# A hybrid attention and state-space layer on one core: the order of TensorE and ScalarE work tied in all blocks of the mixer

## The chip, the cores and the metric

The kernel runs on one core of a Trainium2 chip, in one launch. The metric is the device time of that launch in microseconds, the median of three runs. A core has five engines that run their own instruction streams and meet at semaphores: TensorE (PE; matrix products and transposes, results in PSUM), VectorE (DVE), ScalarE (ACT; functions such as exp and silu, each from a table that an ACT_TABLE_LOAD brings in), GpSimd (POOL), and SyncE (SP), which here issues loads.

## The reference, cut to what matters

The input is x of 4 sequences x 256 positions x 512 channels. Four layers are added to it in turn: attention with an adapter, a gated feed-forward layer, a state-space mixer, and the feed-forward layer again. The change concerns the mixer alone. Cut to its core, the reference of the mixer is

```python
H, P, N, G, K, CS = (128, 64, 128, 8, 4, 32)      # INTER = H * P = 8192
proj = input_states @ in_proj_w.T
gate, xBC, dt = split(proj)
xBC = silu(conv1d(xBC, conv_w, depthwise, K = 4) + conv_b)
hs, Bm, Cm = split(xBC)
A = -exp(A_log); dt = clip(softplus(dt + dt_bias), 0)
cum = cumsum(dt * A)
Ldec = where(i >= j, exp(cum[i] - cum[j]), 0)
scores = einsum('bcihn,bcjhn->bcijh', Cc, Bc) * Ldec * dt
y = einsum('bcijh,bcjhp->bcihp', scores, xc) + (states carried over) + D * hs
g = y * silu(gate)
g = g * rsqrt(mean over a group(g * g) + eps) * norm_w
out = g @ out_w.T
```

The kernel doesn't walk in chunks of 32 with a carried state. It takes the sum over all earlier positions of a sequence at once, with 256 positions as two halves of 128, and so needs, for each head and sequence, three 128 x 128 pieces of decays: first half on itself, second half on the first, second half on itself.

## The kernel before, in words

The mixer has 128 heads of 64 channels. Two heads make a block of 128 channels: 64 blocks (NB). Eight blocks (GB) make a group (G = 8), which shares one pair of projections B and C and one normalisation. All 1024 positions (NT) lie in the free dimension.

Block i of group g, with gi its place in the group, does this:

- `projected("x", i)` (TensorE) multiplies one 128-channel slice of the weights with the input, in two halves of 512 positions. Each half is 4 x 3 matmuls, since `mm3` (lines 110 to 117) makes a float32 product of three products of split parts. The result `pp` lies in PSUM, in a pool of two buffers that x, gate, B and C projections take in turn.
- `conv` (lines 961 to 976): ScalarE writes the bias and one tap from `pp` to `acc` (964), VectorE adds three taps (971), which are the last readers of that `pp`, and ScalarE takes the silu in place (975).
- `projected("g", i)` is the gate, whose silu is `gt` (1219). One `gt` buffer exists.
- `rows` loads a head's cumulated decays from DRAM to all partitions (tile `r`), and `differences` (from 999) makes the three pieces of decays of a head in a tile `em`: four VectorE subtractions (1004), a select on GpSimd (1008), and nine exponentials on ScalarE (1013, 1014, 1016). There are three `em` buffers and a block takes two.
- `weighted` (1020) multiplies `em` with the group's scores `gm` on VectorE.
- `turned` transposes x on TensorE (`trx`, 1027) and scales it by dt on VectorE (`xd`, 1030).
- `product` (1044) multiplies `em` and `xd` to `pyy`, and `gated` (1054, 1057, 1061) adds D x, multiplies with the gate, squares for the norm, and stores the block to DRAM (`spill`).

`scores` (from 977) makes `gm` of a group from its B and C, a sequence at a time, with a PSUM tile `pg` (986, 990) and a VectorE product (991). B and C of the next group are projected in the fourth and fifth block of a group (`NEXT`).

The output product of a group (`recall`, `partial`, `scaled`; tiles `gr`, `gh`, `pog`) is done while the next group runs: eight pieces of 128 positions, 24 matmuls each, dealt to its blocks by the table PER (at the end of block gi, PER[gi + 1] pieces are recalled, and the block after does their products in `outer`).

`trx`, `pg`, `pog` and the sums `pqs` share one PSUM pool of two buffers (tag "m").

What sets the order: each engine's instructions are put in order when the kernel is built, by a scheduler with its own estimate of times. Inside `tc.manual_schedule(engines={nc.tensor.engine})` TensorE keeps the order of the program. Before the change this holds for blocks 8 to 63; the first group and the end after the last block are left to the scheduler. `tc.issue_after(ins)` puts what follows behind `ins` on `ins`'s engine, without a wait between engines.

In a block, TensorE's written order is: first half of x(i), the transposes of block i - 1 (`turn`), second half of x(i), then the product of block i - 1 either at once, or, where `late` is set, between the two halves of the gate's projection.

Of the kernel before, what the change touches and what calls it, by code (L numbers as in the profile page):

```python
# [20 lines left out]
P = 128  # L21
# [12 lines left out]
EPS = 1e-5  # L34

NEXT = {3: "b", 4: "c"}


COLS = {}
# [40 lines left out]
def hybrid_kernel(  # L80
# [705 lines left out]
    def mixer(feed, later):  # L786
        with ExitStack() as es, ExitStack() as inner:
# [168 lines left out]
                    nc.tensor.transpose(tr[:, q, :], dt[:, q * P : (q + 1) * P], ident)  # L956
                nc.scalar.activation(dt_t[:, qs, :], tr, AF.Relu)

            silus = []

            def conv(pp, ch, tag, bufs):

                acc = (po_ if tag == "gb" else p2).tile([P, NT], F32, name="acc", tag=tag, bufs=bufs)
                nc.scalar.activation(  # L964
                    acc, pp, AF.Identity, bias=cb_s[:, ch : ch + 1], scale=cw_s[:, ch, 3:4]
                )
                av = acc.rearrange("p (b t) -> p b t", b=B)
                pv = pp.rearrange("p (b t) -> p b t", b=B)
                for tap in range(3):
                    d = 3 - tap  # L970
                    nc.vector.scalar_tensor_tensor(  # L971
                        av[:, :, d:], pv[:, :, : L - d], cw_s[:, ch, tap : tap + 1], av[:, :, d:],
                        ALU.mult, ALU.add,
                    )
                silus.append(nc.scalar.activation(acc, acc, AF.Silu).ins)
                return acc

            def scores(bt, ct):

                gm = p2.tile([P, B, 3, P], F32, name="gm", tag="gm", bufs=1)  # L980
                yield gm
                for b in range(B):
                    pg = ps.tile([P, 3, P], F32, name="pg", tag="m")
                    k0, k1 = bt[:, b * L : b * L + P], bt[:, b * L + P : (b + 1) * L]
                    q1 = ct[:, b * L + P : (b + 1) * L]
                    nc.tensor.matmul(
                        pg[:, 0:2, :].rearrange("p s i -> p (s i)"), k0, ct[:, b * L : (b + 1) * L],
                        start=True, stop=True,
                    )
                    nc.tensor.matmul(pg[:, 2, :], k1, q1, start=True, stop=True)  # L990
                    nc.vector.tensor_tensor(gm[:, b], pg, tri.rearrange("p (s i) -> p s i", s=3), ALU.mult)
                    yield

            def rows(h):
                r = p2.tile([P, NT], F32, name="r", tag="r", bufs=3)
                load(r, cumd[h : h + 1, :].to_broadcast([P, NT]))
                return r

            def differences(h, r):
# [13 lines left out]
                    nc.scalar.activation(e[:, b, 1, :], rv[:, b, 1, :], AF.Exp, bias=col_t[:, h, b, 2:3])  # L1013
                nc.scalar.activation(e[:, :, 2, :], e[:, :, 2, :], AF.Exp)
                for b in range(B):
                    nc.scalar.activation(e[:, b, 0, :], rv[:, b, 0, :], AF.Exp, bias=col_t[:, h, b, 0:1])  # L1016
                return e

            def weighted(e, gm):
# [77 lines left out]

            def recall(g, t, half):

                r = po_.tile([P, 4, P], F32, name="gr", tag="gr", bufs=3)  # L1100
                s = [po_.tile([P, 4, P], F32R, name=f"gh{j}", tag=f"gh{j}", bufs=3) for j in range(2)]
                ts = slice(t * P, (t + 1) * P)
                n = 3 if half == 1 and g == G - 1 else 4
# [43 lines left out]
            def convolved(kind, g):  # L1147
                at_ = NB if kind == "b" else NB + G
                group[kind] = conv(projected(kind, g), at_ + g, "gb", 3)
# [13 lines left out]
                py = product(xd, em)  # L1163
                sqs[m // GB] = gated(m, px2, gt, py, sqs.get(m // GB))

            convolved("b", 0)
            convolved("c", 0)
            scoring = scores(group["b"], group["c"])
            gm = next(scoring)
            for _ in range(B):  # L1170
                next(scoring)
            rr = {h: rows(h) for h in range(2)}
            stage, sqs, wos, rgs, todo = {}, {}, {}, {}, []
            recalled = []
            PER = {1: 1, 2: 2, 3: 1, 4: 1, 5: 2, 6: 1}
            def block(i, scoring, gm):
                g, gi = divmod(i, GB)
                if gi == 0 and g:
                    scoring = scores(group["b"], group["c"])
                    gm = next(scoring)  # L1180
                    todo.extend((g - 1, t) for t in range(TT))

                def scored():

                    for _ in range(2 if gi == 0 and g else 0):
                        next(scoring)

                def turn():

                    if i - 1 in stage and len(stage[i - 1]) == 3:  # L1190
                        px2, pgt, pem = stage[i - 1]
                        stage[i - 1] = px2, pgt, turned(i - 1, px2), pem

                x2 = conv(projected("x", i, turn), i, "x2", 2)

                late = gi in (7, 0, 1) and g > 0
                if not late:
                    if recalled:  # L1200
                        outer()
                    if i:
                        inner_products(i - 1)
                    while recalled:
                        outer()
                if gi == 6:
                    wos.setdefault(g, []).extend(out_weights(g, k) for k in range(3))

                def between():
                    scored()  # L1210
                    if late:
                        inner_products(i - 1)
                        while recalled:
                            outer()

                pp = projected("g", i, between)
                scored()
                gt = p2.tile([P, NT], F32, name="gt", tag="gt", bufs=1)
                nc.scalar.activation(gt, pp, AF.Silu)
                em = []  # L1220
                for h in (2 * i, 2 * i + 1):
                    with tc.issue_after(silus[2]) if i == 0 else ExitStack():
                        em.append(differences(h, rr.pop(h)))
                    if h + 2 < H:
                        rr[h + 2] = rows(h + 2)
                xd = [turned(i, x2)] if g == 0 else []
                if gi in NEXT and g + 1 < G:
                    convolved(NEXT[gi], g + 1)
                for e in em:
                    weighted(e, gm)  # L1230
                stage[i] = (x2, gt, *xd, em)
                for _ in range(PER.get(gi + 1, 0)):
                    if todo:
                        q, t = todo.pop(0)
                        recalled.append((q, t, [recall(q, t, half) for half in range(2)]))
                if gi == 7:
                    wos[g].extend(out_weights(g, k) for k in range(3, 6))
                if gi == 0 and g:
                    wos[g - 1].extend(out_weights(g - 1, k) for k in range(6, 8))
                return scoring, gm  # L1240

            for i in range(GB):
                scoring, gm = block(i, scoring, gm)
            with tc.manual_schedule(engines={nc.tensor.engine}):
                for i in range(GB, NB):
                    scoring, gm = block(i, scoring, gm)
            px2, pgt, pem = stage[NB - 1]
            stage[NB - 1] = px2, pgt, turned(NB - 1, px2), pem
            inner_products(NB - 1)
            wos[G - 1].extend(out_weights(G - 1, k) for k in range(6, 8))  # L1250
            es_p.close()
            ps_o = pool("m_o", 4, space=PSUM, **freed)
            pos = {}
# [118 lines left out]
```

## Time and profile before

| what | value |
|---|---|
| median of 3 runs | 1888.84 us (1888.56 to 1890.16) |
| the profiled execution, whole | 1889.63 us |
| its span, first to last instruction | 1887.9 us |
| granted TensorE clock, mean | 0.986 |
| table loads on ScalarE in the mixer's silus and exponentials | 60 (line 975), 58 (1219), 49 (1013), 40 (1014), 23 (1016), 1283 ns each |
| first and last product of a block (line 1044) | 426.1 and 1802.3 us |

The profile is of one execution, so its lines are to be set against 1889.63 and not against the median. The span has three stretches: attention and feed-forward up to about 370 us, the mixer's blocks from about 415 to 1803 us, and the last output products with the second feed-forward layer after that. TensorE is called PE, and its weight loads PEld. A busy TensorE means that matmuls are in its pipeline; the ends of matmuls are modelled. In a timeline, the number in brackets is the idle time of that engine before the instruction, and the name after it is what released it. A matmul of 512 columns is shown with 0.39 us, but in a row they start 0.2275 us apart, and in the same way VectorE and ScalarE operations in a row overlap a little, so that start-to-start times are shorter than the durations.

### The profile page before, as it was taken

The page shows a single profiled execution, that of the slowest core. Times are in us where ns is not written, and L with a number is a line of the kernel's source. Part 1 is how long each engine was busy: PE and PEld are TensorE (multiplying, and loading weights), DVE is VectorE, ACT ScalarE, POOL GpSimd, SP SyncE. Part 2 cuts the span into 40 slices and gives each one's busy share as a digit, 9 for nine tenths or more (in the row PEclk, how much of TensorE's full clock was granted, in tenths as well). Part 3 has the DMA queues.
Part 4 walks back from the last instruction along what each step waited for, and adds up shares of the span by engine and source line. Part 5 has one row for each costly group of instructions (what it writes and reads, how often), then busy time and mean ns, then how long its engine had stood idle before and what let it go on. Part 6 is the DMA issues. An engine that isn't in the chain of part 4 may idle for free.

```text
span 1887.9 us, 29843 instructions
## 1 busy us (share of the span) xinstructions
PE 1814.7 (96%) x10706; PEld 1459.8 (77%) x10706; DVE 1470.2 (78%) x2272; ACT 1456.8 (77%) x2876; POOL 465.8 (25%) x425
## 2 busy tenths in 40 slices
PE   8999988899999999999999999999999999999997
PEld 6777767677778887888788878877887888788786
DVE  5566667788888788877878787869787878888767
ACT  6666675379998879887988797879778977988843
POOL 6332230024441122113211311222132222211200
PEclk9999999899999999999999999999999999999999
DMA  4000000035555445543654454546444644554321
GB/s 143 1 1 1 22 15 26 24 102 167 162 181 189 138 145 176 181 143 122 206 156 151 140 185 154 159 125 205 145 146 151 189 140 145 174 176 159 109 91 45
DMA packets 152772, 240.35 MB, mean 127 GB/s; under 512 B 12464, under 2 KB 77616, under 8 KB 152624
## 3 DMA queue, kind: packets, MB, share of 16 engines
q1 hardware_dynamic: 143552, 205.41, 35.1%
q10 hardware_dynamic: 9072, 33.03, 4.5%
q8 instruction: 84, 1.38, 0.3%
q14 instruction: 64, 0.52, 0.1%
HBM read 202.75 MB, written 35.65 MB: 126 GB/s over the span
## 4 chain that ended last, share of the span: by engine, by line
PE 76%; ACT 9%; DVE 8%; issue 3%; POOL 2%; DMA 2%; SPq 0%; ACTq 0%; DVEq 0%; POOLq 0%
PE pp L115 12%; PE pp L116 12%; PE pp L117 11%; PE pyy L1044 9%; PE pog L115 6%; PE pog L116 6%; PE pog L117 6%; PE trx L1027 2%; ACT e L477 2%; DVE acc L971 2%; PE ptr L493 1%; PE pq L115 1%; PE pq L116 1%; PE pq L117 1%; DVE eT L494 1%
## 5 line engine op out<-in xcount | busy, mean ns | idle before, releaser
L115 PE MATMUL pp<-mx,w 128*128 128x512 f32 (+1 forms) x1160 | 463.8, 400 | 4.7 <-DVE acc L971 3.0
L117 PE MATMUL pp<-mx,w 128*128 128x512 f32 (+1 forms) x1160 | 451.9, 390 | 0.0
L116 PE MATMUL pp<-mx,w 128*128 128x512 f32 (+1 forms) x1160 | 451.8, 390 | 0.0
L971 DVE SCALAR_TENSOR_TENSOR acc<-pp,cw_s,acc 128x1012 f32<-128x1012 f32 (+2 forms) x240 | 304.6, 1270 | 47.3 <-ACT acc L964 45.9
L1020 DVE TENSOR_TENSOR em<-em,gm 128x1536 f32<-128x1536 f32 x128 | 229.4, 1792 | 98.8 <-ACT em L1016 94.9
L1008 POOL TENSOR_SCALAR_AFFINE_SELECT r<-r 128x512 f32<-128x512 f32 x128 | 133.0, 1039 | 647.4 <-DMA r<-cumd 553.3
L115 PEld LDWEIGHTS pp<-mx,w 128*128 128x128 f32 x1160 | 218.3, 188 | 58.4 <-issue 7.6
L117 PEld LDWEIGHTS pp<-mx,w 128*128 128x128 f32 x1160 | 218.3, 188 | 46.0 <-issue 0.3
L116 PEld LDWEIGHTS pp<-mx,w 128*128 128x128 f32 x1160 | 218.8, 189 | 40.7 <-issue 0.6
L1068 POOL TENSOR_TENSOR sq<-sq,acc 128x1024 f32<-128x1024 f32 x55 | 147.6, 2684 | 310.7 <-ACT acc L1061 282.6
L115 PE MATMUL pog<-wo,gh 128*128 128x512 f32 x512 | 203.5, 397 | 0.0
L116 PE MATMUL pog<-wo,gh 128*128 128x512 f32 x512 | 200.3, 391 | 0.0
L117 PE MATMUL pog<-wo,gh 128*128 128x512 f32 x512 | 199.9, 390 | 0.0
L1044 PE MATMUL pyy<-em,xd 128*64 128x256 f32 (+1 forms) x2048 | 191.4, 331 | 4.2 <-DVE em L1020 3.0
L1044 PEld LDWEIGHTS pyy<-em,xd 128*64 128x64 f32 x2048 | 135.8, 138 | 64.5 <-issue 20.9
L1004 DVE TENSOR_SCALAR em<-r,col_t 128x128 f32<-128x128 f32 x512 | 169.9, 386 | 14.3 <-PE pyy L1044 13.5
L1013 ACT ACTIVATE em<-r,col_t 128x128 f32<-128x128 f32 x512 | 167.3, 392 | 17.6 <-PE pyy L1044 15.1
L1016 ACT ACTIVATE em<-r,col_t 128x128 f32<-128x128 f32 x512 | 165.4, 388 | 0.3
L107 ACT CAST w<-wr 128x512 fp32r<-128x512 f32 x144 | 88.1, 612 | 69.5 <-PE pp L116 56.4
L1030 DVE TENSOR_TENSOR xd<-trx,dt_t 128x512 f32<-128x512 f32 x128 | 83.2, 683 | 64.9 <-PE trx L1027 64.8
L107 ACT CAST gh<-gr 128x512 fp32r<-128x512 f32 (+1 forms) x128 | 76.7, 605 | 58.4 <-PE pog L116 46.3
L477 ACT ACTIVATE e<-sc,nmx 128x256 f32<-128x256 f32 (+1 forms) x256 | 104.0, 441 | 21.0 <-DVE nmx L471 20.9
(290 smaller groups left out, 3335.3 us busy)
## 6 DMA issues: line engine op xcount, KB each, us to landing
wr<-in_win_dram SPq DMA_DIRECT2D x287, 256.0 KB, 2.8
r<-cumd SPq DMA_DIRECT2D x128, 512.0 KB, 4.1
spill<-gb ACTq DMA_DIRECT2D x63, 512.0 KB, 2.8
gr<-spill SPq DMA_DIRECT2D x120, 256.0 KB, 3.0
wor<-in_wout_dram SPq DMA_DIRECT2D x64, 256.0 KB, 4.0
out_dram<-x SPq DMA_DIRECT2D x8, 256.0 KB, 2.3
x<-in_x_dram SPq DMA_DIRECT2D x1, 1536.0 KB, 8.9
gr<-spill SPq DMA_DIRECT2D x8, 192.0 KB, 2.5
```

Of the source, the lines that this page charges most:

```text
L107: nc.scalar.copy(hl[0], v)
L115: nc.tensor.matmul(o, lh, rh, start=(first and k == 0), stop=False)
L116: nc.tensor.matmul(o, lh, rl, start=False, stop=False)
L117: nc.tensor.matmul(o, ll, rh, start=False, stop=(last and k == n - 1))
L477: nc.scalar.activation(es_[c][:, 2 * j + pr, :], sc[:, j, :], AF.Exp, bias=nm[:, j : j + 1], accum_out=rs[:, c, h : h + 1],)
L971: nc.vector.scalar_tensor_tensor(av[:, :, d:], pv[:, :, : L - d], cw_s[:, ch, tap : tap + 1], av[:, :, d:], ALU.mult, ALU.add,)
L1004: nc.vector.tensor_scalar(e[:, b, 2, :], rv[:, b, 1, :], col_t[:, h, b, 1:2], 0.0, ALU.subtract, ALU.min,)
L1013: nc.scalar.activation(e[:, b, 1, :], rv[:, b, 1, :], AF.Exp, bias=col_t[:, h, b, 2:3])
L1016: nc.scalar.activation(e[:, b, 0, :], rv[:, b, 0, :], AF.Exp, bias=col_t[:, h, b, 0:1])
L1020: nc.vector.tensor_tensor(e, e, gm, ALU.mult)
L1044: nc.tensor.matmul(py[d, b, k * P :], xd[:, 2 * b + k, d], es2[hh][:, b, 2 * k : 2 if k == 0 else 3, :].rearrange("p s i -> p (s i)"), sta ...
L1068: (nc.gpsimd if n < NB - 1 else nc.vector).tensor_tensor(sq, sq, x2, ALU.add)
```

## The change

- All 64 blocks are now under the written order on TensorE, the first group included.
- On ScalarE, the exponentials of block i (both heads) are issued behind the gate's silu of block i - 1; the silu of x(i), with the silu of a B or C made in the block before, behind the last exponential; the gate's silu of block i behind that. `decays(i)` with the loads of the next rows is called ahead of x(i)'s projection.
- The scores of the next group are made in block gi = 6 (the seventh) of a group, two sequences after x's projection and two after the gate's, into one of now two `gm` buffers. Before, they were made in the first block of their group.
- `r` and `gr` go from three to two buffers each.
- In the first group every product is `late`; in the last group the eighth block's is not.
- The last group's turn at output products of the group before follows a new table, LAST: one piece in each block, and the eighth after the last block (`outer()` behind the loop).

```diff
+PER = {1: 1, 2: 2, 3: 1, 4: 1, 5: 2, 6: 1}
+LAST = {1: 1, 2: 1, 3: 1, 4: 1, 5: 1, 6: 1, 7: 1, 8: 1}
...
-            silus = []
+            silus, exps = [], []
+
+            def silu(acc):
+                silus.append(nc.scalar.activation(acc, acc, AF.Silu).ins)
...
-                silus.append(nc.scalar.activation(acc, acc, AF.Silu).ins)
                 return acc
...
-                gm = p2.tile([P, B, 3, P], F32, name="gm", tag="gm", bufs=1)
+                gm = p2.tile([P, B, 3, P], F32, name="gm", tag="gm")
...
-                r = p2.tile([P, NT], F32, name="r", tag="r", bufs=3)
+                r = p2.tile([P, NT], F32, name="r", tag="r", bufs=2)
...
-                    nc.scalar.activation(e[:, b, 0, :], rv[:, b, 0, :], AF.Exp, bias=col_t[:, h, b, 0:1])
+                    exp = nc.scalar.activation(
+                        e[:, b, 0, :], rv[:, b, 0, :], AF.Exp, bias=col_t[:, h, b, 0:1]
+                    )
+                exps.append(exp.ins)
...
-                r = po_.tile([P, 4, P], F32, name="gr", tag="gr", bufs=3)
+                r = po_.tile([P, 4, P], F32, name="gr", tag="gr", bufs=2)
...
+            gms = {}
+
+            def scored(g, n):
+
+                if g == G:
+                    return
+                if g not in gms:
+                    scoring[g] = scores(group["b"], group["c"])
+                    gms[g] = next(scoring[g])
+                for _ in range(n):
+                    next(scoring[g])
...
+            def decays(i):
+                em = []
+                for h in (2 * i, 2 * i + 1):
+                    em.append(differences(h, rr.pop(h)))
+                    if h + 2 < H:
+                        rr[h + 2] = rows(h + 2)
+                return em
+
+            def block(i):
                 g, gi = divmod(i, GB)
+                per = PER if g < G - 1 else LAST
...
+                if i:
+                    with tc.issue_after(silus[-1]):
+                        em = decays(i)
+                x2 = conv(projected("x", i, lambda: turn(i - 1) if i else None), i, "x2", 2)
+                with tc.issue_after(exps[-1]) if i else ExitStack():
+                    for acc in [x2, *unsilued]:
+                        silu(acc)
+                unsilued.clear()
+                if i == 0:
+                    with tc.issue_after(silus[-1]):
+                        em = decays(i)
+                if gi == 6:
+                    scored(g + 1, 2)
 
-                late = gi in (7, 0, 1) and g > 0
+                late = g == 0 or (gi in (7, 0, 1) and g < G - 1) or gi < 2
...
                 pp = projected("g", i, between)
-                scored()
+                if gi == 6:
+                    scored(g + 1, 2)
                 gt = p2.tile([P, NT], F32, name="gt", tag="gt", bufs=1)
-                nc.scalar.activation(gt, pp, AF.Silu)
-                em = []
-                for h in (2 * i, 2 * i + 1):
-                    with tc.issue_after(silus[2]) if i == 0 else ExitStack():
-                        em.append(differences(h, rr.pop(h)))
-                    if h + 2 < H:
-                        rr[h + 2] = rows(h + 2)
-                xd = [turned(i, x2)] if g == 0 else []
+                with tc.issue_after(silus[-1]):
+                    silus.append(nc.scalar.activation(gt, pp, AF.Silu).ins)
                 if gi in NEXT and g + 1 < G:
                     convolved(NEXT[gi], g + 1)
+                    unsilued.append(group[NEXT[gi]])
                 for e in em:
-                    weighted(e, gm)
-                stage[i] = (x2, gt, *xd, em)
-                for _ in range(PER.get(gi + 1, 0)):
+                    weighted(e, gms[g])
+                stage[i] = (x2, gt, em)
+                for _ in range(per.get(gi + 1, 0)):
...
-            for i in range(GB):
-                scoring, gm = block(i, scoring, gm)
             with tc.manual_schedule(engines={nc.tensor.engine}):
-                for i in range(GB, NB):
-                    scoring, gm = block(i, scoring, gm)
-            px2, pgt, pem = stage[NB - 1]
-            stage[NB - 1] = px2, pgt, turned(NB - 1, px2), pem
+                for i in range(NB):
+                    block(i)
+            outer()
+            turn(NB - 1)
             inner_products(NB - 1)
```

## The prediction

> **What bounds the kernel now.** I read the page's busy shares first, then TensorE's own table of waits, then the timelines of TensorE, VectorE and ScalarE around one group start (904 to 930 us), last the end of the block loop.
>
> ```profile
> span 1887.9 us, 29843 instructions
> PE 1814.7 (96%) x10706; PEld 1459.8 (77%) x10706; DVE 1470.2 (78%) x2272; ACT 1456.8 (77%) x2876; POOL 465.8 (25%) x425
> ```
>
> TensorE is the bound. From 919.04 to 1098.43 us, one group of eight blocks (179.4 us), it is busy 178.1 us, ScalarE 148.2, VectorE 147.8. Its waits in the mixer are few:
>
> ```profile
> PE pg L986 <- DVE gm L991: 8.6, 7, 1.4
> PE pyy L1044 <- DVE em L1020: 3.0, 3, 2.2
> PE pp L115 <- DVE acc L971: 3.0, 4, 1.5
> ```
>
> The columns are total us, times, longest. The first is the seven group starts, where the scores wait for the single gm. All TensorE gaps over 0.05 us from 418 us to the loop's end add up to about 19 us: 8.6 there, 5.4 in the first group, 4.6 in the last block, the rest tiny. That is all that better order could win directly.
>
> Now a group start (block 24), ScalarE, then VectorE, then TensorE:
>
> ```profile
> 911.62 1.20 ACT L964 ACTIVATE acc<-pp,cb_s,cw_s 128x1024 f32<-128x1024 f32 x1
> ...
> 916.94 1.26 ACT L1013 ACTIVATE em<-r,col_t 128x128 f32<-128x128 f32 x4
> 918.11 0.97 ACT L1016 ACTIVATE em<-r,col_t 128x128 f32<-128x128 f32 x3
> 919.10 1.28 ACT L975 ACT_TABLE_LOAD   x1
> ```
>
> ```profile
> 917.25 1.27 DVE L971 SCALAR_TENSOR_TENSOR acc<-pp,cw_s,acc 128x1020 f32<-128x1020 f32 x1
> ...
> 919.37 1.27 DVE L1054 SCALAR_TENSOR_TENSOR gb<-acc,dh,pyy 128x1024 f32<-128x1024 f32 x1
> ```
>
> ```profile
> 912.05 2.82 PE L1044 MATMUL pyy<-em,xd 128*64 128x256 f32 x32
> ...
> 919.04 0.70 PE L986 MATMUL pg<-acc 128*128 128x256 f32 x2 [1.21 <-DVE gm L991]
> ...
> 920.37 0.48 PE L115 MATMUL pp<-mx,w 128*128 128x512 f32 x1
> ```
>
> The reader is to see an order: the bias of x's convolution (911.62) comes before the second head's exponentials, which wait for the product of the block before (912.05 to 914.80). So the last convolution tap, begun at 917.25, is over at 918.5, before TensorE wants that PSUM buffer for the next block's x (920.37).
>
> [...] a load from 907.76 is followed by an exponential at 909.06. [...] after the 2.20 us gap before 1798.15 the clock is 0.50 in 1798.6 to 1802.0, and at 1793 us matmuls stand 0.43 us apart, not 0.227.
>
> **The change, part by part.** I took instruction order from the built program, durations from the trace. Rn is block n's transposes, Yn its product.
>
> (a) Table loads fall from 262 to 165: 97 x 1.283 = 124 us of ScalarE. I count 0: ScalarE has 31 us to spare in a group, and after the first group no TensorE wait for it in the block loop exceeds 0.1 us until the last block.
>
> (b) Scores in block 6 with two gm, their VectorE products (0.55 us each) moving along: the waits go, -8.6. The first product of a group also ran 3.40 us instead of 2.75 (929.63 to 933.03) on late weighted exponentials: 7 x 0.65 = -4.5. New: the scores share two PSUM buffers with transposes and out products, and stand behind weighted multiplies on VectorE. By hand gm is ready within 0.2 us of need: +1.5 for seven (0 to +7).
>
> (c) The decisive part. Each block takes two of three em buffers, so a block's second head waits for the preceding product. At blocks 16, 24, 32, 40, 48 and 56 the built ScalarE order is now (block 16; em_8113 is its second head, acc_8178 its convolution):
>
> ```
> 721 L1019 Activation em_8113<-r_7962,col_t_4980 128x128 x4
> 722 L1020 Activation em_8113<-em_8113 128x4x128
> 723 L1022 Activation em_8113<-r_7962,col_t_4980 128x128 x4
> 724 L111 TensorCopy w0_8136<-wr_7966 128x512
> 725 L971 Activation acc_8178<-pp_8140,cb_s_4737,cw_s_4735 128x1024
> ```
>
> So the convolution's bias, and a weight cast for the next x, are queued behind exponentials that wait for Y15, and Y15 stands in the middle of g16. VectorE has the same inversion: second head's differences, gated, first head's weighting, a weight's low part, the gate's multiply, and only then the taps. TensorE's x17 takes x16's PSUM buffer, so it waits for the third tap. Counted from Y15's end, in back-to-back starts of the VectorE timeline: 0.1 semaphore (898.40 to 898.50 between Y's end and an exponential); differences 0.87; gated 1.19; weighting 1.67; low part 0.60; multiply 1.14; tap 1.19; low part 0.60; tap 1.19; weighting 1.67; tap 1.27 = 11.5 us. ScalarE stays inside this: exponentials 1.18 + 0.52 + 1.27, cast 0.5, bias 1.2 end at 4.8; tap one starts at 5.6. TensorE has only g16's second half, 12 x 0.2275 = 2.7 us. Stall 8.7 us, six times: +52. R16's silu (tap, load 1.28, silu 1.06: 13.9) is then in time, x17's half ending at 14.3. Block 8 keeps the bias ahead and is counted in (e).
>
> (d) [...] 6 x 1.6 = +9.6 (0 if the clock holds[...]).
>
> (e) First group, now tied. Before: gaps 5.4 us, and seven products cut after two matmuls, each restart about 0.4: -8 in all. After, the third tap stands behind the second head's differences: in block 2 x3 waits 4.2 us (0.97 + tap 1.19 + gated 1.19 + tap 1.19 + multiply 1.14 + tap 1.27 = 7.0, less 2.7); by the same sums block 8 3.7, block 7 1.9, block 6 1.7 (there R6 waits for gm), and Y0 about 1 without filling matmuls. +12.5[...]. Net +7 (-5 to +15).
>
> (f) The end. An out product now covers the last silu: -1.4 - 1.1 - 2.2, and the two half-clock windows there -3.2. The last product still waits for its transposes scaled on VectorE behind weight work, about +1.2[...]. Net -5.
>
> (g) r from three to two buffers, gr likewise. A row is free when its exponentials end, about 11 us before the next use; landing takes a median 4.1 us and the select 1.04. gr lands in 3.0. Rows and selects move up with the exponentials. On SP a row's load waits for exponentials and holds weight loads behind it, which are wanted a block later; on POOL square sums (2.68 us) stand behind selects that wait for rows, and the next reader of their tile comes some 10 us later. I take 0 (0 to +10). Silus behind exponentials reach R at 5.5 us after Y in blocks with 5.56 us of cover: +1 in all (0 to +10).
>
> Sum: -8.6 - 4.5 + 1.5 + 52 + 9.6 + 7 - 5 + 1 = +53. The profiled execution took 1889.63 us (span 1887.9 and 1.7 around it): 1942.6. The median, 1888.84, is 0.8 lower: I say 1942.
>
> **Rivals.** *Faster:* the tie works as named, with no inversion. Then (c), (d) and (e)'s stalls vanish and -8.6 - 4.5 + 1.5 - 5 - 8 + 1 = -24: about 1866. For it: TensorE waits on little else, and ScalarE gains 124 us. Against: the listed order, em's three buffers. It decides if x17's wait after Y15 is under 3 us, for then six waits are under 18 us. *Stalls without the clock, cheap first group:* drop (d), (e) at 0: 53 - 17 = +36, about 1925. [...] *More waits:* the tight silus and the two-buffer loads of (g) at their upper ends[...]: +53 + 9 + 10 + 9 = +81, 1970. Against: 8 to 14 us of cover in most blocks. *The tie does nothing:* excluded for order, since the built orders differ; but equal time would need gains and stalls to cancel, 2%.
>
> **How the numbers follow.** Forecast 0.71, stalls without clock 0.14, more waits 0.08, faster 0.05, same 0.02. The range, 1918 to 1964, takes the forecast with (d) and (e) at their bounds and the second rival, and leaves most of the third and all of the faster one out. What a measurement can tell from no change is 0.2%: faster 0.05, same 0.02, slower 0.93.
>
> **What would show it.** TensorE's waits should name the convolution taps (pp from acc) with six waits near 8.7 us, each at a group's second x; the clock should read a half just after; pg's wait should be gone; ACT_TABLE_LOADs should be 165 and ScalarE's busy time near 1330. Wrong if those six waits are short: then the order of execution or the buffer's owner isn't what I read. Groups of 179.4 us should become about 188.

## The result, and the profile after

| | us | ratio to before, 95% interval |
|---|---|---|
| before, median of 4 runs (the three above and one more) | 1888.70 (1886.68 to 1890.16) | |
| after, median of 4 runs | 1952.26 (1949.57 to 1955.48) | 1.0338 [1.0317, 1.0359] |
| after, the profiled execution (span 1948.4) | 1950.19 | |

The change costs 63.6 us. The forecast was 1942, its range 1918 to 1964. The page's busy shares first:

```profile
span 1948.4 us, 29707 instructions
PE 1816.9 (93%) x10706; PEld 1461.4 (75%) x10706; DVE 1487.7 (76%) x2272; ACT 1330.1 (68%) x2779; POOL 448.2 (23%) x425
```

TensorE does the same 10706 matmuls in nearly the same busy time (2.2 us more), so nearly all of the loss is idleness. ScalarE is busy 127 us less and nothing is gained by it. TensorE's table of waits (total us, times, longest):

```profile
PE pp L119 <- DVE acc L978: 71.4, 10, 10.3
PE trx L1036 <- DVE gm L997: 4.3, 2, 2.4
...
PE pog L119 <- DVE gm L997: 1.9, 6, 0.3
```

The wait for gm ahead of the scores is gone; projections now wait for the taps of a convolution (978). Six of the ten are at x(17), x(25), ... x(57), 10.1 to 10.3 us each. Timelines around the first of them, ScalarE, then VectorE (whole from 741.44 on), GpSimd and TensorE:

```profile
741.44 1.29 ACT L1019 ACTIVATE em<-r,col_t 128x128 f32<-128x128 f32 x4 [0.78 <-PE pyy L1053]
742.63 0.62 ACT L1020 ACTIVATE em<-em 128x512 f32<-128x512 f32 x1
743.15 1.28 ACT L1022 ACTIVATE em<-r,col_t 128x128 f32<-128x128 f32 x4
744.33 0.61 ACT L111 CAST w<-wr 128x512 fp32r<-128x512 f32 x1
744.84 1.21 ACT L971 ACTIVATE acc<-pp,cb_s,cw_s 128x1024 f32<-128x1024 f32 x1
```

```profile
741.44 0.88 DVE L1010 TENSOR_SCALAR em<-r,col_t 128x128 f32<-128x128 f32 x4 [1.17 <-PE pyy L1053]
742.23 1.28 DVE L1063 SCALAR_TENSOR_TENSOR gb<-acc,dh,pyy 128x1024 f32<-128x1024 f32 x1
743.42 1.75 DVE L1029 TENSOR_TENSOR em<-em,gm 128x1536 f32<-128x1536 f32 x1
745.09 0.69 DVE L112 TENSOR_TENSOR w<-wr,w 128x512 fp32r<-128x512 f32 x1
745.69 1.22 DVE L1066 TENSOR_TENSOR gb<-gb,gt 128x1024 f32<-128x1024 f32 x1
746.83 1.27 DVE L978 SCALAR_TENSOR_TENSOR acc<-pp,cw_s,acc 128x1012 f32<-128x1012 f32 x1
748.01 0.68 DVE L112 TENSOR_TENSOR w<-wr,w 128x512 fp32r<-128x512 f32 x1
748.61 1.27 DVE L978 SCALAR_TENSOR_TENSOR acc<-pp,cw_s,acc 128x1016 f32<-128x1016 f32 x1
749.79 3.32 DVE L1029 TENSOR_TENSOR em<-em,gm 128x1536 f32<-128x1536 f32 x1
753.04 1.27 DVE L978 SCALAR_TENSOR_TENSOR acc<-pp,cw_s,acc 128x1020 f32<-128x1020 f32 x1
```

```profile
749.16 2.34 POOL L1077 TENSOR_TENSOR sq<-sq,acc 128x1024 f32<-128x1024 f32 x1
```

```profile
743.96 0.39 PE L121 MATMUL pp<-mx,w 128*128 128x512 f32 x1
754.45 0.77 PE L119 MATMUL pp<-mx,w 128*128 128x512 f32 x1 [10.10 <-DVE acc L978]
755.02 0.63 PE L120 MATMUL pp<-mx,w 128*128 128x512 f32 x1
```

The reader is to see the inversion in two queues. On ScalarE the second head's exponentials wait for Y15 (released at 741.44 by pyy), and the bias of x(16) stands behind them (744.84), although the matmuls of x(16) were over before 736 and ScalarE stood idle for 0.78 us just ahead of 741.44. On VectorE the three taps stand behind and between seven other operations, 9.2 us from start to start, of which the first waits for Y15 too. VectorE doesn't pause until the last tap ends at 754.3, and the bias was over at 746.05, 0.8 us ahead of the first tap: so it is VectorE's queue that sets the length of the stall. Had the taps (3.6 us) followed the bias at once, the last would have ended at about 749.7; by this estimate from the lines above ScalarE's order alone would still leave some 5 of the 10.1 us. TensorE is out of work at 744.35 and idles for these 10.1 us. Behind the wait its matmuls take 0.63 us instead of 0.39, at a granted clock of 0.50 up to 758.8.

The span in sections, by the ends of the products (us; Yn is block n's product):

| | to the mixer | Y0 to Y8 | six groups, Y8 to Y56 | Y56 to Y63 | Y63 to the end |
|---|---|---|---|---|---|
| before | 407.8 | 142.1 | 179.4 to 179.7 | 151.7 | 85.2 |
| after | 402.4 | 151.3 | 189.4 to 190.8 | 142.9 | 85.3 |

The 24.4 us from the start of the mixer to Y0 are the same in both. The six groups bring +65.5, the first +9.2, the last stretch -8.8. The 5.4 us ahead of the mixer are not the change's: over all profiles of this study that stretch took 401.8 to 407.8 us with the same code.

### The profile page after: what moved, and what is told of

It reads as the page before. It is cut to its first block, busy times and chain, and to the rows that moved or that the text cites. A ratio compares the mean times of both kernels' runs of the same rounds, so it can differ in the third digit from the quotient of the medians.

```text
span 1948.4 us, 29707 instructions
## 1 busy us (share of the span) xinstructions
PE 1816.9 (93%) x10706; PEld 1461.4 (75%) x10706; DVE 1487.7 (76%) x2272; ACT 1330.1 (68%) x2779; POOL 448.2 (23%) x425
## 4 chain that ended last, share of the span: by engine, by line
PE 74%; DVE 12%; ACT 7%; issue 3%; DMA 2%; POOL 2%; SPq 0%; DVEq 0%; ACTq 0%; POOLq 0%
PE pp L119 12%; PE pp L120 11%; PE pp L121 11%; PE pyy L1053 8%; PE pog L119 6%; PE pog L120 6%; PE pog L121 6%; DVE acc L978 3%; PE trx L1036 2%; ACT e L481 2%; DVE em L1029 2%; PE ptr L497 1%; PE pq L119 1%; DVE em L1010 1%; PE pq L120 1%
## 5 line engine op out<-in xcount | busy, mean ns | idle before, releaser
L119 PE MATMUL pp<-mx,w 128*128 128x512 f32 (+1 forms) x1160 | 472.3, 407 | 72.6 <-DVE acc L978 71.4
L120 PE MATMUL pp<-mx,w 128*128 128x512 f32 (+1 forms) x1160 | 458.8, 396 | 0.0
L121 PE MATMUL pp<-mx,w 128*128 128x512 f32 (+1 forms) x1160 | 457.9, 395 | 0.0
L119 PEld LDWEIGHTS pp<-mx,w 128*128 128x128 f32 x1160 | 222.7, 192 | 126.7 <-issue 76.7
L1014 POOL TENSOR_SCALAR_AFFINE_SELECT r<-r 128x512 f32<-128x512 f32 x128 | 119.8, 936 | 765.2 <-DMA r<-cumd 588.3
L1029 DVE TENSOR_TENSOR em<-em,gm 128x1536 f32<-128x1536 f32 x128 | 238.7, 1865 | 43.1 <-ACT em L1022 42.6
L121 PEld LDWEIGHTS pp<-mx,w 128*128 128x128 f32 x1160 | 222.8, 192 | 47.9
L120 PEld LDWEIGHTS pp<-mx,w 128*128 128x128 f32 x1160 | 223.4, 193 | 41.3
L1077 POOL TENSOR_TENSOR sq<-sq,acc 128x1024 f32<-128x1024 f32 x55 | 136.5, 2482 | 264.3 <-ACT acc L1070 264.3
L1053 PE MATMUL pyy<-em,xd 128*64 128x256 f32 (+1 forms) x2048 | 180.5, 329 | 0.7 <-DVE xd L1039 0.7
L1053 PEld LDWEIGHTS pyy<-em,xd 128*64 128x64 f32 x2048 | 128.1, 137 | 60.3 <-issue 18.3
L1010 DVE TENSOR_SCALAR em<-r,col_t 128x128 f32<-128x128 f32 x512 | 146.1, 342 | 25.8 <-PE pyy L1053 22.9
L112 DVE TENSOR_TENSOR gh<-gr,gh 128x512 fp32r<-128x512 f32 (+1 forms) x128 | 103.2, 815 | 44.0 <-ACT gh L111 44.0
```

The source lines that it names most:

```text
L119: nc.tensor.matmul(o, lh, rh, start=(first and k == 0), stop=False)
L120: nc.tensor.matmul(o, lh, rl, start=False, stop=False)
L121: nc.tensor.matmul(o, ll, rh, start=False, stop=(last and k == n - 1))
L1010: nc.vector.tensor_scalar(e[:, b, 2, :], rv[:, b, 1, :], col_t[:, h, b, 1:2], 0.0, ALU.subtract, ALU.min,)
L1014: nc.gpsimd.affine_select(rv[:, :, 0, :], rv[:, :, 0, :], pattern=[[0, B], [1, P]], compare_op=ALU.is_ge, fill=-1e30, base=0, channel_mult ...
L1029: nc.vector.tensor_tensor(e, e, gm, ALU.mult)
```

## The experiments

The sums named below are those six. Each ratio is to executions of the kernel before that were taken along with the run (medians 1888.25 to 1890.34), and each "theory" is one that the expectation of that run names. For the reading, the mean interval from one product's end to the next, by place in the group (groups 2 to 6 counted from 0; place 0 is from Y15 to Y16, place 7 from Y14 to Y15, and likewise in the other groups):

| us | 0 | 1 | 2 to 4, each | 5 | 6 | 7 |
|---|---|---|---|---|---|---|
| before | 18.29 | 24.76 | 25.63 | 25.63 | 17.47 | 16.42 |
| after | 27.36 | 24.76 | 25.63 | 27.56 | 18.83 | 14.77 |
| scores alone | 18.27 | 24.77 | 25.63 | 27.26 | 18.83 | 15.13 |
| both heads behind the conv | 15.40 | 25.27 | 25.63 | 27.55 | 18.83 | 19.64 |
| the same, old scores | 16.13 | 24.76 | 25.63 | 25.63 | 17.47 | 20.65 |
| the same, no ties | 16.45 | 24.76 | 25.63 | 25.63 | 17.47 | 18.23 |
| 43 filling products | 25.35 | 24.76 | 25.63 | 27.66 | 18.83 | 14.75 |

**1. The second head's exponentials behind the conv.**

```diff
-                        em = decays(i)
+                        em = decays(i, (0,))
                 x2 = conv(...)
+                bias, tap = convs[-1]
+                if i:
+                    with tc.issue_after(bias), tc.issue_after(tap), tc.issue_after(exps[-1]):
+                        em += decays(i, (1,))
```

> The changed kernel, with one thing moved: the second head's exponentials (and its clamp and its mask) are built behind the same block's conv bias and last tap instead of ahead of them. The ties between exponentials and silus, the scores in block 6, the two-buffer r and gr and the new dealing of out products stay; 206 table loads instead of 165. In blocks 16, 24, ... 56 only the gated sum of the product before still stands between two taps. Theory 1 (the inversion is the loss: a stall of 10.1 us and about 2 us of halved clock at each of six places): the wait ahead of the next x projection falls from 10.1 to about 1.6 us, the clock stays full there, and the six sums of eight blocks fall from 190.5 to about 180 us: 1880 to 1890 us in all, level with the kernel before. Theory 2 (the ties, or fewer buffers for r and gr, or a tighter order in general cost the time): the six sums stay above 187 us and the time above 1930.

Measured: 1973.59 us, 1.0451 [1.0429, 1.0473]; six sums 191.5 to 193.7. The 10 us wait is gone, but 2.2, 1.1, 1.4 and 4.0 us came at four places nearby. By its numbers theory 2 came true, but the run was no clean test: the first head's exponentials, still called ahead, keep the bias behind them, and 41 table loads came on top. ScalarE's timeline, and the same 16 us in the windows of this run and of the kernel before (columns: busy TensorE, weight loads, VectorE, ScalarE, GpSimd, then clock, DMA share, GB/s):

```profile
753.06 1.28 ACT L1020 ACTIVATE em<-r,col_t 128x128 f32<-128x128 f32 x4
...
755.93 1.19 ACT L971 ACTIVATE acc<-pp,cb_s,cw_s 128x1024 f32<-128x1024 f32 x1
```

```profile
744.00:760.00 16.00, 12.83 (x77) 9.36 (x76) 9.54 (x9) 15.90 (x30) 3.02 (x3) 0.97 0.58 165
```

```profile
744.00:760.00 16.00, 15.95 (x96) 12.75 (x95) 16.00 (x21) 15.92 (x31) 3.68 (x2) 1.00 0.76 236
```

The projection of x(16) was over about 749, its bias began at 755.93. ScalarE is full in both kernels here; before, TensorE doesn't wait, as the bias comes early in the queue. Order decides here, not ScalarE's busy share.

**2. The taps in a row as well.**

```diff
+                with tc.issue_after(convs[-1][1]) if m < NB - 1 else ExitStack():
-                sqs[m // GB] = gated(m, px2, gt, py, sqs.get(m // GB))
+                    sqs[m // GB] = gated(m, px2, gt, py, sqs.get(m // GB))
```

> As the run with the second head's exponentials behind the conv, and besides, the gated sum of the product before is tied behind the last tap of the block's x conv on VectorE, so that nothing stands between the taps of blocks 16, 24, ... 56; 233 table loads. Theory 1 (the inversion is the whole loss): no wait before the six x projections, sums of eight blocks of 178 to 179 us, 1868 to 1880 us in all: faster than the kernel before, by what the other parts of the change bring. Theory 2 (ties, buffers or lost freedom of order): above 1930 us. In between, at 1885 to 1930, both carry a part.

Measured: 1966.38 us, 1.0413 [1.0389, 1.0437]; six sums 188.1 to 190.6. By its numbers theory 2 again. Waits of 1.2, 1.0 and 5.1 us are left around Y15. The 5.1 us are at x(17), where the bias (756.44) still stands behind the first head's exponentials (the last four from 754.76). Moving one head is no cure, even with the taps together.

**3. Both heads behind the conv.** A clean test: TensorE's order is unchanged.

```diff
-                if i:
-                    with tc.issue_after(silus[-1]):
-                        em = decays(i)
                 x2 = conv(projected("x", i, lambda: turn(i - 1) if i else None), i, "x2", 2)
+                if i:
+                    with tc.issue_after(silus[-1]):
+                        em = decays(i)
```

> The changed kernel with one call moved: both heads' exponentials are called behind the x conv of their block instead of ahead of it. Ties, scores in block 6, two-buffer r and gr and the dealing of out products stay, TensorE's order is the same to the instruction, there are 166 table loads for 165. In blocks 16, 24, ... 56 the conv bias now stands ahead of both heads' exponentials on ScalarE and the three taps stand in a row on VectorE. (The earlier run with the second head alone moved was no clean test: it left the first head's nine exponentials ahead of the bias and added 41 table loads.) Theory 1 (the inversion in six blocks is what costs): no waits of 10 us, the six sums 179 to 182 us, 1870 to 1892 us in all. Theory 2 (the ties or the two-buffer tiles cost): six sums above 187 us, above 1935 us. Between: both.

Measured: 1909.06 us, 1.0116 [1.0101, 1.0131]; six sums 183.0 to 184.6. TensorE's waits:

```profile
PE trx L1036 <- ACT acc L966: 26.5, 13, 3.6
PE pp L119 <- DVE acc L978: 5.0, 7, 1.0
```

The waits for taps fall from 71.4 to 5.0 us and 43 us are won. That is most of the loss, but the kernel stays 21 us above before: between the theories. What comes late now is the silu of x (966), which the tie puts behind all exponentials.

**4. The old place of the scores, with both heads behind the conv.**

```diff
-                if gi == 6:
-                    scored(g + 1, 2)
+                if gi == 0 and g:
+                    scored(g, 2)
```

(at both places, with one gm and three r and gr)

> As the run with both heads' exponentials behind the conv, and the scores put back where the kernel before has them (a group's first block, one buffer for gm, three for r and gr); 178 table loads. If moving the scores costs about 2 us a group, as it did alone on the kernel before: 8 to 14 us below the run with both heads behind the conv. If in the company of the ties the move does bring the waits for gm: 5 to 12 us above it.

Measured: 1894.21 us, 1.0035 [1.0023, 1.0047], 14.9 us less than experiment 3. So the moved scores cost, together with the two-buffer r and gr that go with them. In the table of intervals places 5 and 6, where the moved scores were, shrink by 1.9 and 1.4 us, and 7 and 0 grow by 1.0 and 0.7. The first group is 5.3 us shorter.

**5. The scores moved, alone on the kernel before.**

```diff
-                if gi == 0 and g:
+                if gi == 6 and g + 1 < G:
                     scoring = scores(group["b"], group["c"])
...
-                    for _ in range(2 if gi == 0 and g else 0):
+                    for _ in range(2 if gi == 6 and g + 1 < G else 0):
```

(two gm, two r and gr; half of the scores ahead of the out products, as in the change)

> The kernel before with one part of the change alone: a group's scores computed in the seventh block of the group before (two buffers for gm, two instead of three for r and gr). Theory 1 (as the prediction's step on the scores has it): the waits for gm and the slow products behind them in the first block of a group go, 8.6 us and 4.5 us, about 1.5 us of small waits come: 11 us less, about 1877 us. Theory 2 (two buffers for r and gr, or two score products ahead of the out products, take it back): 1886 us or more.

Measured: 1901.59 us, 1.0062 [1.0050, 1.0075]: 11.3 us slower, theory 2 and the opposite of the prediction's step. TensorE's timeline at the group start:

```profile
740.65 0.47 PE L115 MATMUL pp<-mx,w 128*128 128x512 f32 x1 [1.43 <-DVE acc L971]
748.60 0.50 PE L115 MATMUL pp<-mx,w 128*128 128x512 f32 x1 [1.13 <-ACT gt L1222]
```

The wait for gm (1.2 us) went, and these two came. In the table of intervals, places 5 and 6, where TensorE never waited, grow by 1.63 and 1.36 us, the scores' own matmuls; place 7 gives back 1.29; place 0 gives nothing. The two new waits are for VectorE and ScalarE, so around the group start TensorE is held by these, and the scores had been filling that time. Fewer buffers for r and gr went along and weren't tried apart.

**6. The old place of the scores in the changed kernel.** The same edit, on the changed kernel.

> The changed kernel with only the scores put back where the kernel before has them (one buffer for gm, three for r and gr); 159 table loads. The conv bias of block 16 then stands ahead of the second head's exponentials, but in block 17 all nine exponentials of the second head, which wait for block 16's product, stand ahead of block 17's bias. Theory 1 (the early call of the exponentials makes an inversion, wherever the order puts it): a wait of about 10 us moves one block on, to the projection x(18), x(26), ...; 1930 to 1955 us. Theory 2 (moving the scores is what makes the stall): no wait above 3 us, under 1905 us.

Measured: 1914.56 us, 1.0151 [1.0131, 1.0170]: neither theory.

```profile
PE pp L119 <- DVE acc L978: 31.7, 11, 5.4
```

No 10 us wait is left. TensorE waits for taps 2.0 us at x(17) and not at all at x(18), where theory 1 had the stall, so theory 1 is refuted there. But the first group takes 159.4 us (before 142.1), and five waits for taps of 1.0 to 5.4 us, 18.7 of the 31.7, lie in it. With the old scores ScalarE has the bias of block 16 (748.66) ahead of the second head's exponentials (750.27) again: the inversion there takes the early call together with the moved scores and the buffers that go with them.

**7. The ties removed, the early call kept.** The three `issue_after` inside the blocks are left out.

```diff
-                    with tc.issue_after(silus[-1]):
-                        em = decays(i)
+                    em = decays(i)
...
-                with tc.issue_after(exps[-1]) if i else ExitStack():
-                    for acc in [x2, *unsilued]:
-                        silu(acc)
+                for acc in [x2, *unsilued]:
+                    silu(acc)
...
-                with tc.issue_after(silus[-1]):
-                    silus.append(nc.scalar.activation(gt, pp, AF.Silu).ins)
+                silus.append(nc.scalar.activation(gt, pp, AF.Silu).ins)
```

> The changed kernel without its three ties inside the blocks (exponentials after the last silu, silus after the last exponential, the gate's silu after the last silu); exponentials are still called ahead of the x conv. The table loads rise from 165 to 256, which is 117 us more of ScalarE time at 1.28 us a load. ScalarE still has the second head's exponentials ahead of the conv bias in blocks 16, 24, ... 56. Theory 1 (what costs is where the exponentials are called, and table loads lie beside TensorE's work): the six stalls of about 10 us remain, the time stays within 8 us of the changed kernel, 1945 to 1962 us. Theory 2 (the ties cost the time): under 1915 us. Theory 3 (fewer table loads do pay, hidden by the stalls): above 1975 us.

Measured: 1957.96 us, 1.0368 [1.0348, 1.0388]: as theory 1 has it in time, with 91 more table loads, though not in the size of the stalls. They change their shape: 6.1 us, named by the gate's silu, then 0.8 to 1.9 us at the transposes, and 1.8 us at out products in five groups. Without the ties, the early call and the moved scores (with the two-buffer tiles) still make the loss.

**8. The ties removed from run 4.**

> As the run with both heads behind the conv and the old scores, with the three ties removed as well; table loads rise from 178 to 268. What is left of the change is the call of the exponentials just behind the x conv, the silu taken out of the conv's code, and the new dealing at the end. Theory 1 (the tie costs, because it holds the x silu, which the transposes of the next block wait for, behind all exponentials of the block: 20 us of waits for it in the run with ties): 1876 to 1887 us, in spite of 90 more table loads. Theory 2 (the ties are free, and what is left above the run of the new dealing alone comes of the other rearrangement): 1891 us or more.

Measured: 1883.85 us, 0.9979 [0.9969, 0.9988]. Theory 1. Five of the six sums are 178.9 to 179.0, one is 181.2. Without the ties 10 us are won in spite of 90 more table loads. In the two profiles the six groups are 12.7 us shorter, the first group 5.0 and the stretch behind Y63 6.2 us longer; whether the table loads have a part in these two isn't shown. TensorE's waits for the x silu and for the gate's silu (with ties, then without):

```profile
PE trx L1036 <- ACT acc L966: 20.1, 10, 3.5
PE pp L119 <- ACT gt L1254: 8.2, 5, 2.7
```

```profile
PE pp L119 <- ACT gt L1251: 15.0, 10, 2.6
PE trx L1036 <- ACT acc L966: 3.5, 3, 2.0
```

**9. The new dealing of out products, alone on the kernel before.**

```diff
-            for _ in range(PER.get(gi + 1, 0)):
+            for _ in range((PER if g < G - 1 else LAST).get(gi + 1, 0)):
...
+            outer()
             px2, pgt, pem = stage[NB - 1]
```

(with the change's `late` for the last group)

> The kernel before with one part of the change alone: the last group's out products dealt one to a block, one of them kept until after block 63. Theory 1: the waits and the halved clock of blocks 57 to 63 go in part, as in the changed kernel (where blocks 56 to 63 took 142.9 instead of 151.7 us): 5 to 9 us less, 1880 to 1884 us. Theory 2 (in the changed kernel the ties or the earlier exponentials made those blocks shorter): within 2 us of 1888.7.

Measured: 1879.00 us, 0.9943 [0.9930, 0.9956], 11 us less: theory 1, slightly more than it said. Y56 to Y63 take 144.7 us instead of 151.7. It beats both kernels, and is the best of all runs.

**10. Filling products in the gap: what the clock costs.**

```diff
+                if gi == 0 and g:
+                    warmed(ps.tile([P, C], F32, name="warm", tag="m"), [ones] * 32)
```

> The changed kernel with 32 products of 128x128 on the constant ones (0.275 us each, 8.8 us in all, result unread) issued behind the g projection of each group's first block but the first group's, which is in the idle time of 10.1 us ahead of the next x projection. Theory 1 (the idle time halves the clock[...], which costs 2.1 us a place): the wait of TensorE shrinks to 1 to 1.5 us, the x projection behind it starts at the same time as before but runs at full clock, half of it in 2.8 us instead of 4.9, and the time falls by 10 to 13 us to about 1940. Theory 2 (the slow products behind the wait come of something else, or VectorE is what is late, so that a faster TensorE only waits later): within 3 us of 1952.

Measured: 1948.95 us, 1.0322 [1.0296, 1.0348]. The products took 0.228 us each, not 0.275, so waits of 3.0 to 3.3 us were left. Behind the one at x(17), 2.97 us before 761.57, the clock fell to a half again: matmuls of 0.63 us from the third on. The time fits neither theory; hence the same with 43:

> As the run with 32 filling products behind the g projection of a group's first block, with 43 of them: at the 0.228 us each that they took there, 9.8 us of the 10.3. (With 32 a wait of 3.0 us was left, and the x projection behind it still ran its products at 0.63 instead of 0.39 us.) Theory 1 (idle time of TensorE is what halves the clock): the wait left is under 0.8 us, the products behind it take 0.39 to 0.40 us each, and each of the six sums falls by about 2 us against the changed kernel: 1938 to 1944 us. Theory 2 (the slow products have another cause): they stay at 0.63 us, and the time at 1948 to 1953 us.

Measured: 1946.26 us, 1.0301 [1.0280, 1.0322]; six sums 188.0 to 188.8: theory 1 in the waits and the matmuls, with a time 2 us above what it gave. TensorE's timeline at x(17), which the longer first group puts at another time:

```profile
762.35 0.47 PE L119 MATMUL pp<-mx,w 128*128 128x512 f32 x1 [0.81 <-DVE acc L978]
762.66 0.40 PE L120 MATMUL pp<-mx,w 128*128 128x512 f32 x1
```

The half of x(17) behind the wait takes 2.82 us; in the changed kernel it takes 4.87 (754.45 to 759.32). The halved clock thus costs 2.05 us there, 1.4 to 2.4 us at the six places if 2.82 is set against each half, 13.0 in all, and the six sums fall by 12.8 together. The whole falls by 6 only, since the first group is 6.6 us longer: block 8 gets the filling products too, and its wait was 3.46 us, so that 9.8 us of them push x(9) back by 6.3. The length of one wait doesn't decide here: in the changed kernel 1.90 us before 532.44 were followed by a clock of 0.51 from 533.5 to 536.9, and 3.46 us before 566.03 by 1.00 throughout; the wait of 0.81 us before 762.35 here left it full (matmuls of 0.39 to 0.40 us).

**11. Without GpSimd's sum of squares at the stall.**

```diff
-                if not first:
+                if not first and (n % GB < GB - 1 or n == NB - 1):
                     (nc.gpsimd if n < NB - 1 else nc.vector).tensor_tensor(sq, sq, x2, ALU.add)
```

> The changed kernel without GpSimd's sum of squares of the last block of each group (one addition of 128x1024 in eight left out, so the norm of each group lacks an eighth of its channels); all orders are otherwise the same. In the changed kernel this addition ran beside VectorE's weighting of the second head's factors, which took 3.32 us there instead of 1.75, within the chain that the six stalls wait for. Theory 1 (the two engines slow each other, the addition is the cause): the weighting takes about 1.75 us and the six waits 8.5 instead of 10.1 us; the time falls by 8 to 10 us to about 1943. Theory 2 (the slow weighting has another cause, such as the transfers of that moment): waits of 10.1 us, time within 2 us of 1952.

Measured: 1938.10 us, 1.0263 [1.0247, 1.0279]; six sums 187.7 to 187.8. VectorE's timeline, then TensorE's:

```profile
751.63 1.75 DVE L1029 TENSOR_TENSOR em<-em,gm 128x1536 f32<-128x1536 f32 x1
```

```profile
754.72 0.77 PE L119 MATMUL pp<-mx,w 128*128 128x512 f32 x1 [8.53 <-DVE acc L978]
```

Theory 1, and more than it said: the weighting takes 1.75 us instead of 3.32, the wait is 8.5 instead of 10.1, and the half of x(17) behind it 4.21 instead of 4.87. The six shorter waits make 9.7 of the 15.7 us that the six sums fall. The rest fits the clock, which is at half for about 2.9 us behind the wait at x(17) here (mean of 0.70 from 754.7 to 759.6), against 4.4 at x(17) and 3.1 to 6.2 at the six places in the changed kernel; whether the shorter wait or only its place in time brings that isn't shown. In the changed kernel GpSimd's sum runs from 749.16 to 751.50 and the weighting beside it from 749.79 to 753.11; how the one slows the other isn't shown.

## Why the prediction was right, point by point

**The total.** 1942 was said, 1952 came: in the range, by the likeliest case. What it named came: 165 table loads, ScalarE busy for 1330.1 us, six waits that name the taps, a half clock behind them. Steps (b) to (d) together were +50 for the groups; the six groups brought +65.5. Of the 15 us between the two, some 12 are the sizes of (c) and (d); the rest isn't accounted for. The end, 3.8 us better than said, and the stretch ahead of the mixer, 5.4 us shorter in the profile with the same code, hid a part of it.

**(a) Table loads at no gain: right, with a limit.** Experiments 7 and 8 changed their number by 90 and showed nothing near 115 us. But the 31 us to spare in a group are not spread evenly: in the 16 us around the group start ScalarE had 0.1 us to spare before the change.

**(b) The scores, -11.6: wrong as a part.** What the step named came true in the changed kernel: the wait for gm and the slow first product are gone. But it booked the gap as a gain without asking what would be late next. Alone the move costs 11 us (experiment 5), where the slow first product also stays (3.6 to 3.8 us), and it costs 15 us beside the conv-first order (experiment 4), both times with the buffers that go with it. Inside the changed kernel the stall hides this, as a stall counted from Y15 swallows what TensorE saves there.

**(c) The inversion, 8.7 us six times: right in place and mechanism, short by 1.4 us each.** Every VectorE step of the sum came within 0.1 us except one: the second weighting, 1.67 in the sum, took 3.25 start to start, because GpSimd's sum of squares ran beside it (experiment 11). The prediction took its 1.67 from the weighting at 897.12, beside which GpSimd did nothing (its next instruction began at 901.64). That ScalarE keeps the order of its queue, on which the step rests, shows in the bias: its input was there before 736, and it began at 744.84, behind the exponentials. Experiment 3 confirms the step: with the order put right and TensorE's own order unchanged, the waits for taps fall from 71.4 to 5.0 us.

**(d) The half clock, 1.6 us each: right in kind, 1.4 to 2.4 measured** (experiment 10). The 1.6, and the upper bound of 19 for all six that is in the range, were estimates; from the kernel before, with a clock of 0.50 from 1798.6 to 1802.0 and matmuls 0.43 instead of 0.227 us apart, 1.6 is 3.4 x (1 - 0.227/0.43). In the changed kernel the clock stayed at 0.50 for 3.1 to 6.2 us behind the waits. How long a wait has to be for it wasn't shown.

**(e) First group, +7: +9.2 measured.** The waits came where they were said: x3 4.9 us for 4.2, R6 1.9 for 1.7, x8 1.7 for 1.9, x9 3.5 for 3.7. The rest fits the clock, at half for some 10 us of this stretch (0.50 from 448.2 to 455.0, 0.51 from 533.5 to 536.9), for which the net of +7 had 3 us, the author's estimate.

**(f) The end, -5: -8.8 measured from Y56 to Y63, -7.0 there with the dealing alone.** The half clock that the -3.2 stands for was there before, 0.50 from 1791.8 to 1795.1 and from 1798.6 to 1802.0; in the changed kernel it is 1.00 from 1840 to 1874. The new wait is 0.7 us, not 1.2, and the 1.6 us of half clock behind it that are in the net of -5, an estimate, didn't come.

**(g) Buffers and silus, +1: too low where the inversion is absent.** The x silu behind all exponentials costs 10 us once it is what comes late (experiments 4 and 8). In the changed kernel the stalls covered it.

**The rival "faster" at 1866** rested on (b) and on ties at no cost. With the inversion gone the change is still 21 us slower (experiment 3). A chain of edits splits the 63.6 us in order: inversion 43 (after to experiment 3), scores with their buffers 15 (to 4), ties 10 (to 8), 5 for what else differs from experiment 9, less 10 for the dealing (experiment 9 to before). That these add up is no evidence, since each step starts where the last one ended. The shares hold for this chain alone; taken in another order they differ, as experiment 6 shows, where the scores put back in the changed kernel win 38.

**Open:** what the 5 us between experiments 8 and 9 are made of, which order brings the waits of the first group in experiment 6, and what the two-buffer r and gr cost by themselves.

## What to carry to other kernels

An engine's queue is where this reordering cost most (43 of 63.6 us, experiment 3): look for what each instruction of a chain that frees a buffer (here the bias on ScalarE and the taps on VectorE) is put behind, and whether that waits for the very engine that needs the buffer. A wait of TensorE is no gain to be had until the next late input is known (8.6 us for gm in the kernel before, but the move alone cost 11); work that fills a stretch held by other engines, as the scores did, was nearly free there (18.29 us with them, 18.27 without) and cost its full 1.63 and 1.36 us where TensorE never waited (experiment 5). Try each part of a change alone: here one part of three gained 11 us and was buried under the others.

## What the runs showed of the hardware

- VectorE's product of two tiles (128x1536) took 3.32 us beside a GpSimd addition that had begun 0.6 us earlier, and 1.75 without it (changed kernel and experiment 11). Without the addition six groups were 15.7 us shorter, 9.7 of them in the waits.
- TensorE at half clock: matmuls of 128x512 took 0.63 us instead of 0.39, at a granted clock of 0.50 (changed kernel, 754.45 to 758.8). Which single wait brings it can't be read from its length in these runs: 1.90 us (before 532.44, changed kernel) did, 3.46 us (before 566.03, the same) didn't. It also set in after the restart: in the kernel before, TensorE went on at 1798.15 and the clock was 1.00 up to 1798.6, then 0.50 up to 1802.0.
- The stretch before the mixer, with the same code, took 407.8 us in the profile before and 402.4 in the one after, so a difference of 5 us in one section between two single profiles is no finding there.
